# Row convolutions four rows at a time, six tiles of exponentials added in DRAM, one bank drained by VectorE

## The chip, the cores and the metric

One core of one Trainium2 chip runs the whole kernel. The metric is the device time of one execution in microseconds (us); three runs of the kernel before gave a median of 1929.07 us (1928.27 to 1931.76).

## The reference

Eight images of 64 channels and 64 x 64 pixels pass two layers.

```python
# layer 0: attention over the 4096 pixels of each image, plus a unary term
q, k, v = wq @ x + bq, wk @ x + bk, wv @ x + bv
q, k = q - mean(q), k - mean(k)
out = softmax(q.T @ k / 8) applied to v
out = out + sum over pixels of softmax(mean(q) . k) * v
x = x + out
# layer 1: three binary convolutions of the same x, summed, gated
s = sum over k in (1, 3, 5) of batchnorm(conv(sign(x + move_k), mean|w_k| * sign(w_k - mean w_k)) + cb_k)
gate = sigmoid(grouped product of mean(s) over pixels with gw, + gb), channels shuffled
return s * gate + x
```

Signs are +1 and -1, so each convolution is a sum of small integers, times one factor per output channel.

## The kernel before, in words

Images are worked in four pairs: 128 partitions are 64 channels of one image and 64 of the other. A pair has eight blocks of 512 pixels (8 rows of the image), so the kernel has 32 blocks, numbered g. A block has 32 steps, numbered j; each takes 128 pixels as keys.

**A step** (`scores`, `weighted`, `summed`; loop in `attend`). TensorE (PE) makes the scores of both images, four fp32 products of 64 x 64 weights and 512 columns, one in each quarter of its array. ScalarE (ACT) takes their exponential out of PSUM into a tile e (`L485`), 128 x 1024 fp32; e comes from a pool `ep` of five buffers, which it shares with the gather's tile `parts`. One step later PE multiplies e by the values (`L493`) into the two banks `acc`, and VectorE (DVE) adds e to `es` (`L506`, `L508`). Every fp32 product is two instructions on PE. Scores use a ring of two double banks of PSUM (`ps_s`), `acc` has one pair (`ps_a`), and everything else shares two banks (`ps_m`, `m_tile`).

**What hangs on the steps.** `plan(g)` gives each step of block g a list of further work; every engine takes its instructions in the order in which the program emits them, and DMAs issued on SP or POOL are taken in order too. At step 0 of a block:
- `weighted_out` (`L516`): ACT copies both banks of the block before to SBUF;
- `send` (`L523`) and `gather` (`L531`): es goes to DRAM and comes back in another arrangement, in four transfers on SP; `fold_first`, `fold`, `fold_last` and `spread` (steps 3 to 6) add the rest, take reciprocals and send them to all partitions; `added`, `finish` (12, 13) make the layer's output; `signs_wide`, `signs` (15, 17, 19) its signs;
- `mix_rows`: on PE, the queries of the next block (`L460`) and the convolutions of the block three before.

**The convolutions, two rows at a time.** `row_sums` and `row_sums3` (steps 17 and 19) make sums and differences of rows of signs on VectorE; SP copies what the other half of the partitions needs. Products (`row_product`, `L704`) then work on half as many rows: A, B, S and D, four for 3x3 of 3 taps each; for 5x5 A, B and S with 10 taps and D with 5. One product has 64 x 64 bf16 weights and 256 columns (four rows of 64). The order on PE is made in `mix_rows`: one sequence for each half of the partitions (row group), the two images side by side; the 3x3 follows eight of the products of S and the 1x1 (`L787`). `begin_rows` (`L730`) and `hold_rows` (`L737`) on ACT take the 1x1 and the 3x3 out of PSUM at the end of `mix_rows`; `add_rows` (`L746`, `L752`) on DVE adds the 5x5, `add_halves` (`L759`) and `end_rows` (`L765`) follow at steps 7 to 10.

The weights of S and D are made once, in block 2 (`weight_combinations`). The last block and what comes after it use another path (`mix`), one product for each tap. The values of the next pair (`values`, `L313`) are made in the second half of a pair's blocks.

Of the kernel before, what the change touches and what calls it, by code (L numbers as in the profile page):

```python
# [26 lines left out]
P = 128  # L27
# [12 lines left out]
FIRST = [0, 1, 10, 35]  # L40
LOW, HIGH = 1e-20, 1e20
# [3 lines left out]
def conv_seq_kernel(ctx, tc, x, wq, wk, wv, vecs, w1, w3, w5, wtap, gw, out):  # L45
# [44 lines left out]
    def load_weights():  # L90
# [7 lines left out]
        for h in range(2):  # L98
# [22 lines left out]

    wc = {
        k: cp.tile([P, k // 2 + 1, k * C], BF16, tag=f"wc{k}", name=f"wc{k}") for k in KS[1:]
    }


# [5 lines left out]
            cp.tile([P if o == 0 else C, HH + k - 1, HH + k - 1], BF16, tag=f"s{k}{o}", name=f"s{k}{o}")  # L132
            for o in range(2 if k == 3 else 1)
# [62 lines left out]
    frac = {k: cp.tile([P, 3], F32, tag=f"frac{k}", name=f"frac{k}") for k in KS[1:]}  # L196
# [3 lines left out]
    def norms():  # L200
        nc.vector.reciprocal(inv, inv)
        nc.vector.tensor_tensor(inv, inv, gamma, ALU.mult)
        nc.vector.tensor_tensor(scale, inv, sf, ALU.mult)
        for n in (1, 2):
            for i, f in enumerate((0.5, -0.5, -1.0)):
                nc.vector.tensor_scalar(
                    frac[KS[n]][:, i : i + 1], scale[:, n : n + 1], f, None, ALU.mult
                )
        nc.vector.tensor_tensor(sh3, cb, rm, ALU.subtract)
        nc.vector.tensor_tensor(sh3, sh3, inv, ALU.mult)  # L210
        nc.vector.tensor_tensor(sh3, sh3, beta, ALU.add)
        nc.vector.tensor_reduce(shift, sh3, AX.X, ALU.add)
# [32 lines left out]
    def n_products(k, name):  # L245
        return k if k == 3 or name == "D" else 2 * k

    def weight_combinations(k):
        tt, w, g = nc.vector.tensor_tensor, wc[k], [tap_row(k, r) for r in range(k)]
        tt(w[:, 1, :], g[0], g[2], ALU.add)  # L250
        tt(w[:, 0, :], w[:, 1, :], g[1], ALU.add)
        tt(w[:, 1, :], g[1], w[:, 1, :], ALU.subtract)
        if k == 5:
            tt(w[:, 2, :], g[3], g[4], ALU.add)
            nc.vector.tensor_scalar(w[:, 2, :], w[:, 2, :], 2.0, None, ALU.mult)

    class Pair:
# [3 lines left out]
        def __init__(self, name, xt):  # L261
            self.name, self.x = name, xt
            self.xs = sm.tile([P, 8], F32, tag="xs", name=f"xs_{name}")
            self.q, self.x2, self.s, self.y1, self.acc = {}, {}, {}, {}, {}
            self.es, self.r, self.joint, self.sc, self.gap = {}, {}, None, None, None
# [235 lines left out]
        def summed(self, qb, j, e):  # L501
            if j == 0:
# [7 lines left out]
        def weighted_out(self, qb, parts=(slice(0, QB),)):  # L510

            acc = self.acc[qb]
            self.acc[qb] = self.tile(fp, "o", qb, (P, 2, QB))
            for c in parts:
                for h in range(2):
                    nc.scalar.copy(self.acc[qb][:, h, c], acc[h][:, c])  # L516
# [3 lines left out]

        def send(self, qb):
            self.sent = self.tile(dp, "es", qb, (4, 32, 4, QB // 2))
            nc.sync.dma_start(  # L523
                out=self.sent.rearrange("g i q c -> (g i) (q c)"),
                in_=self.es.pop(qb).rearrange("p b c -> p (b c)"),
            )
# [52 lines left out]
        def added(self, qb, cols=slice(0, QB)):  # L579
# [3 lines left out]
            nc.vector.tensor_tensor(self.x2[qb][:, cols], acc[:, 0, cols], acc[:, 1, cols], ALU.add)  # L583
# [12 lines left out]
        def join(self):  # L596
# [32 lines left out]
        def copy_tile(self):  # L629
# [3 lines left out]
            for r in (0, W5 - 2):  # L633
                nc.vector.memset(self.sc[:, r : r + 2, :], 0.0)

        def copy_signs(self, qb, n, r0, r1, copies):
            rows = slice(qb * ROWS + r0 + pads[n], qb * ROWS + r1 + pads[n])
            for b in range(2):
                if self.sc is not None and n == 2:
                    copies[b](out=self.sc[img[1 - b], rows, :], in_=sy[n][0][img[b], rows, :])  # L640
                elif self.sc is not None and b == 1:
                    copies[b](out=sy[n][1][:, rows, :], in_=sy[n][0][img[b], rows, :])
# [7 lines left out]
        def row_sums(self, qb):  # L650


            r0 = qb * ROWS
            tt, y5 = nc.vector.tensor_tensor, sy[2][0]
            e5 = self.tile(fp, "e5", qb, (P, 22, W5), BF16)
            e3 = self.tile(fp, "e3", qb, (P, 16, W3), BF16)


            ec = self.tile(fp, "ec", qb, (P, 8 * W5 + 16 * W3), BF16)
            c0 = ec[img[0], 0 : 8 * W5].rearrange("p (r w) -> p r w", w=W5)  # L660
            c1 = ec[img[1], 0 : 18 * W5].rearrange("p (r w) -> p r w", w=W5)
            c3 = ec[img[0], 8 * W5 :].rearrange("p (r w) -> p r w", w=W3)
            self.rows_of_sums = e5, e3, c0, c1, c3
            tt(e5[:, 0:8, :], y5[:, r0 : r0 + 8, :], y5[:, r0 + 2 : r0 + 10, :], ALU.subtract)
            tt(e5[:, 8:18, :], y5[:, r0 + 1 : r0 + 11, :], y5[:, r0 + 2 : r0 + 12, :], ALU.subtract)
            tt(e5[:, 18:22, :], y5[:, r0 + 1 : r0 + 8 : 2, :], y5[:, r0 + 2 : r0 + 9 : 2, :], ALU.add)
            nc.sync.dma_start(out=c1, in_=e5[img[0], 0:18, :])
            nc.sync.dma_start(out=c0[:, 0:4, :], in_=e5[img[1], 18:22, :])
            nc.sync.dma_start(out=c0[:, 4:8, :], in_=y5[img[1], r0 + 4 : r0 + 11 : 2, :])

        def row_sums3(self, qb):
            r0 = qb * ROWS
            tt, y3 = nc.vector.tensor_tensor, sy[1][0]
            _, e3, _, _, c3 = self.rows_of_sums
            tt(e3[:, 0:8, :], y3[:, r0 : r0 + 8, :], y3[:, r0 + 2 : r0 + 10, :], ALU.subtract)
            odd, even = y3[:, r0 + 1 : r0 + 8 : 2, :], y3[:, r0 + 2 : r0 + 9 : 2, :]
            tt(e3[:, 8:12, :], odd, even, ALU.subtract)
            tt(e3[:, 12:16, :], odd, even, ALU.add)
            nc.sync.dma_start(out=c3, in_=e3[img[1]])

        def row_product(self, z, b, k, name, i, r0):

            e5, e3, c0, c1, c3 = self.rows_of_sums
            half, c = divmod(i, k)
            h = 1 if k == 5 and name != "S" else 0
            taps = {
                "A": (tap_row(k, 0), tap_row(k, min(3, k - 1))),
                "B": (tap_row(k, 2), tap_row(k, k - 1)),
                "D": (wc[k][:, 1, :],),
                "S": (wc[k][:, 0, :], wc[k][:, k // 2, :]),  # L690
            }[name][half]
            if k == 3:
                first, step = {"A": (0, 2), "B": (1, 2), "D": (8, 1), "S": (12, 1)}[name]
                src = e3[img[0]] if b == 0 else c3
            elif h == 1:
                first, step = {"A": (0, 10), "B": (1, 11), "D": (8,)}[name][half], 2
                src = e5[img[1]] if b == 1 else c1
            elif b == 1:
                first, step, src = 4 * half, 1, c0
            elif half == 0:  # L700
                first, step, src = 18, 1, e5[img[0]]
            else:
                first, step, src = r0 + 4, 2, sy[2][0][img[0]]
            nc.tensor.matmul(  # L704
                z[img[b], :].rearrange("p (h w) -> p h w", w=HH),
                taps[img[h], c * C : c * C + C],
                src[:, first : first + 3 * step + 1 : step, c : c + HH],
                start=(i == 0),
                stop=(i == n_products(k, name) - 1),
# [12 lines left out]
        def row_sets(self, qb):  # L722

            sv = self.s[qb].rearrange("p (j t w) -> p j t w", t=2, w=HH)
            return sv[:, :, 0, :], sv[:, :, 1, :]

        def begin_rows(self, qb, z):

            self.s[qb] = self.sum_tile(qb)
            nc.scalar.activation(self.s[qb], z, AF.Identity, bias=shift, scale=scale[:, 0:1])  # L730

        def hold_rows(self, qb, two, i):

            if i == 0:
                self.zh, self.z3 = self.tile(sm, "es", f"z3_{qb}", (P, 2, QB)), []
            z = self.zh[:, i, :]
            nc.scalar.activation(z, two, AF.Identity, scale=frac[3][:, 0:1])  # L737
            self.z3 += [
                z[:, bass.ts(t, QB // 2)].rearrange("p (j w) -> p j w", w=HH) for t in range(2)
            ]  # L740

        def add_rows(self, qb, a, b, s):

            for out, z, by in zip(self.row_sets(qb), (a, b), (scale[:, 2:3], frac[5][:, 2:3])):
                z = z.rearrange("p (j w) -> p j w", w=HH)
                nc.vector.scalar_tensor_tensor(out, z, by, out, ALU.mult, ALU.add)  # L746
            self.join_halves(2, s)

        def join_halves(self, i, z):
            t = self.z3[i]  # L750
            z = z.rearrange("p (j w) -> p j w", w=HH)
            nc.vector.scalar_tensor_tensor(t, z, frac[5][:, 0:1], t, ALU.mult, ALU.add)  # L752

        def add_halves(self, qb, i):

            if i == 3:
                self.join_halves(3, self.z5d)
            for t, out in enumerate(self.row_sets(qb)):
# [536 lines left out]
```

## Time and profile before

| what | value |
|---|---|
| median of three runs | 1929.07 us |
| the profiled execution | 1928.49 us, of which the span 1926.3 |
| granted TensorE clock | 0.997 |
| exponentials on ACT, `L485` | 1024 of 1024 ns |
| additions to es on DVE, `L508` | 960 of 1220 ns |
| row products on PE, `L704` | 2726 of 270 ns, overlapping |
| scores and weighted products on PE | 8192 and 8192 instructions of 590 ns, overlapping |
| DMA | 80.58 MB, one queue busy 13.1% of 16 engines' span |

The span goes from the first to the last instruction; the profiled execution's time has 2.2 us around it. Matmuls are pipelined, so the duration of one on PE is not what it costs: four of them run at once in quarters of the array, and the next starts before one ends. How often they start is read from the timeline. A row of the timeline is start, duration, engine, line, operation, output and input, count.

### The profile page before, as it was taken

The numbers are of one execution on the slowest core, as the hardware profiler recorded it, in microseconds if no ns is written. First come the engines' busy times: TensorE is split into PE (matmuls) and PEld (weight loads), VectorE is DVE, ScalarE is ACT, GpSimd is POOL, SyncE is SP. The second block draws the span as 40 slices with busy tenths as digits, with TensorE's granted clock in tenths as the row PEclk, the third lists the DMA queues.
The fourth block names the chain that finished last, engine by engine and source line by source line (L and its number), as shares of the span: only waits on it lengthen the run. The fifth ranks groups of instructions, "written<-read, shape, count | busy, mean of one in ns | idle before, by whom it ended". The sixth has DMA issues, their size and how long they took to land.

```text
span 1926.3 us, 48418 instructions
## 1 busy us (share of the span) xinstructions
PE 1908.6 (99%) x20848; PEld 954.7 (50%) x20848; DVE 1592.5 (83%) x2066; ACT 1277.6 (66%) x1585; POOL 5.9 (0%) x26
## 2 busy tenths in 40 slices
PE   9999999999999999999999999999999999999997
PEld 4333544444356453454435545444544555666664
DVE  6878888889887888888888888898887888877876
ACT  5667766666666766666666676666666666666663
POOL 0000000000000000000000000000000000000000
PEclk9999999999999999999999999999999999999998
DMA  3021110110102111111101211011111011111011
GB/s 101 32 65 33 30 40 32 40 35 16 41 32 84 57 49 29 41 32 40 35 15 41 81 56 57 27 30 41 32 40 35 16 57 48 52 39 39 23 35 46
DMA packets 58998, 80.58 MB, mean 42 GB/s; under 512 B 15628, under 2 KB 40600, under 8 KB 58648
## 3 DMA queue, kind: packets, MB, share of 16 engines
q1 hardware_dynamic: 58024, 76.22, 13.1%
q8 instruction: 165, 2.70, 0.6%
q10 hardware_dynamic: 720, 1.18, 0.2%
q14 instruction: 57, 0.47, 0.1%
q0 software_dynamic: 32, 0.01, 0.0%
HBM read 39.27 MB, written 24.77 MB: 33 GB/s over the span
## 4 chain that ended last, share of the span: by engine, by line
PE 97%; DVE 1%; ACT 1%; DMA 0%; issue 0%; SPq 0%; DVEq 0%
PE ps L474 46%; PE acc L493 45%; PE z L704 4%; PE pv L313 1%; PE pq L460 1%; PE z L787 1%; DMA x<-in_x 0%; ACT e L485 0%; DVE es L508 0%; PE z_5d L704 0%; PE warm L155 0%; DVE r L577 0%; DVE sb L829 0%; ACT rc_ck L418 0%; DVE es_j L829 0%
## 5 line engine op out<-in xcount | busy, mean ns | idle before, releaser
L485 ACT ACTIVATE e<-ps 128x1024 f32<-128x1024 f32 x1024 | 1048.5, 1024 | 605.4 <-PE ps L474 588.8
L508 DVE TENSOR_TENSOR es<-es,e 128x1024 f32<-128x1024 f32 x960 | 1171.5, 1220 | 182.3 <-ACT e L485 152.9
L474 PE MATMUL ps<-q,x 64*64 64x512 f32 x8192 | 1136.7, 590 | 0.9 <-DVE kb L165 0.9
L493 PE MATMUL acc<-e,v 64*64 64x512 f32 x8192 | 1133.8, 589 | 0.6 <-ACT e L485 0.3
L474 PEld LDWEIGHTS ps<-q,x 64*64 64x64 f32 x8192 | 434.7, 133 | 407.4 <-issue 190.8
L493 PEld LDWEIGHTS acc<-e,v 64*64 64x64 f32 x8192 | 379.1, 131 | 501.3 <-ACT e L485 301.6
L704 PE MATMUL z<-ec,wt 64*64 64x256 bf16 x754 | 69.1, 270 | 0.0
L704 PE MATMUL z<-e,wt 64*64 64x256 bf16 x754 | 69.1, 270 | 0.0
L746 DVE SCALAR_TENSOR_TENSOR sb<-z,scale,sb 128x256 f32<-128x256 f32 x29 | 14.0, 484 | 65.7 <-PE z L704 65.7
L704 PEld LDWEIGHTS <-wt 64*64 64x64 bf16 x1508 | 65.0, 105 | 0.1
L506 DVE TENSOR_TENSOR es<-e,e 128x1024 f32<-128x1024 f32 x32 | 39.2, 1226 | 26.8 <-ACT e L485 26.8
L704 PE MATMUL z<-ec,wc 64*64 64x256 bf16 x464 | 60.5, 270 | 0.0
L704 PEld LDWEIGHTS <-wc 64*64 64x64 bf16 x1218 | 57.5, 106 | 3.1
L620 ACT ACTIVATE s<-x,vec 128x512 bf16<-128x512 f32 (+2 forms) x66 | 46.2, 702 | 5.1 <-DVE x L588 5.1
L759 DVE TENSOR_TENSOR sb<-sb,es_z 128x256 f32<-128x256 f32 x116 | 43.9, 420 | 1.0
L704 PE MATMUL z<-e,wc 64*64 64x256 bf16 x319 | 44.4, 270 | 0.0
L737 ACT ACTIVATE es_z<-z,frac 128x512 f32<-128x512 f32 x58 | 39.1, 687 | 0.0
L516 ACT COPY o<-acc 128x512 f32<-128x512 f32 (+2 forms) x66 | 34.4, 580 | 1.2 <-PE acc L493 1.2
L313 PEld LDWEIGHTS pv<-wx,x 64*64 64x64 f32 x1024 | 23.6, 134 | 15.8 <-issue 8.2
L467 DVE TENSOR_SCALAR q<-pq,mx 128x256 f32<-128x256 f32 x30 | 14.5, 484 | 19.7 <-PE pq L460 19.7
L704 PE MATMUL z<-s,wc 64*64 64x256 bf16 x145 | 25.4, 270 | 0.0
L588 DVE SCALAR_TENSOR_TENSOR x<-x,ou,x 128x512 f32<-128x512 f32 (+2 forms) x33 | 24.3, 736 | 1.2
(156 smaller groups left out, 752.6 us busy)
## 6 DMA issues: line engine op xcount, KB each, us to landing
es<-es SPq DMA_DIRECT2D x31, 512.0 KB
e_parts<-es SPq DMA_DIRECT2D x124, 128.0 KB
r<-rc SPq DMA_DIRECT2D x62, 128.0 KB
x<-in_x SPq DMA_DIRECT2D x15, 512.0 KB
out<-sb SPq DMA_DIRECT2D x28, 256.0 KB
ec<-e SPq DMA_DIRECT2D x29, 153.0 KB
xc<-in_x SPq DMA_DIRECT2D x60, 64.0 KB
ec<-e SPq DMA_DIRECT2D x29, 132.0 KB
```

What stands on the lines that cost most here:

```text
L313: nc.tensor.matmul(pv[img[h], b, i * w : (i + 1) * w], self.x[img[b], bass.ds((4 * g + i) * P + h * H, H)], self.wx[img[b], :], start=True ...
L474: nc.tensor.matmul(ps[img[h], b, :], self.x[img[b], bass.ds(j * P + h * H, H)], self.q[qb][img[b], :], start=True, stop=neg is None,)
L485: nc.scalar.activation(e, ps, AF.Exp, scale=1.0 / 8.0)
L493: nc.tensor.matmul(self.acc[qb][h][img[b], :], self.v[img[h], j, img[b]], e[img[h], b, :], start=(j == 0), stop=(j == NK - 1),)
L506: nc.vector.tensor_tensor(self.es[qb], self.first, e, ALU.add)
L508: nc.vector.tensor_tensor(self.es[qb], self.es[qb], e, ALU.add)
L516: nc.scalar.copy(self.acc[qb][:, h, c], acc[h][:, c])
L588: nc.vector.scalar_tensor_tensor(x2, x2, self.ou, self.x[:, bass.ts(qb, QB)][:, cols], ALU.add, ALU.add)
L620: nc.scalar.activation(sy[n][0][:, rows, pad : pad + HH], self.x2[qb][:, r0 * HH : r1 * HH].rearrange("p (h w) -> p h w", w=HH), AF.Sign, ...
L704: nc.tensor.matmul(z[img[b], :].rearrange("p (h w) -> p h w", w=HH), taps[img[h], c * C : c * C + C], src[:, first : first + 3 * step + 1 ...
L737: nc.scalar.activation(z, two, AF.Identity, scale=frac[3][:, 0:1])
L759: nc.vector.tensor_tensor(out, out, self.z3[i], ALU.subtract if (i, t) == (3, 1) else ALU.add)
```

## The change

**Four rows at a time.** Four output rows come from combinations of six (3x3) or eight (5x5) rows of signs, and as many products of 3 or 5 taps, each with combined weights. A product now has 128 columns: 64 pixels of the first and the second four rows of the block. The factors are small whole numbers, exact in bf16; the fractions (1/24, 1/360, 1/45) lie in the scale on the way out. `row_sums` becomes `row_step` in seven parts on VectorE (steps 17 to 24), with copies at 21 and 24. Out of PSUM: `hold` on ACT (3x3, and products 4 and 5 of the 5x5), `join` on DVE, then `sums_of_pairs`, `odd_powers` (ACT), `end_products`, `add_pair` at steps 2 to 9. `begin_rows` moves to step 1, the folds and `spread` two steps later, the unary products and the means' scores from step 0 to step 1.

**Sums in DRAM.** In blocks 0 to 30, tiles 4, 9, 14, 19, 24 and 28 of e aren't added by VectorE. The first is written to DRAM by SP; the others, and then es, are added to it there by transfers that POOL issues.

**One bank by VectorE.** `weighted_out` copies the second bank on DVE.

```diff
+DRAM_TILES = (4, 9, 14, 19, 24, 28)
...
-        def summed(self, qb, j, e):
-            if j == 0:
+        def summed(self, qb, j, e, dram=False):
+            if dram and j in DRAM_TILES:
+                self.add_in_dram(qb, e, j == DRAM_TILES[0])
+            elif j == 0:
...
-                for h in range(2):
-                    nc.scalar.copy(self.acc[qb][:, h, c], acc[h][:, c])
+                nc.scalar.copy(self.acc[qb][0][:, c], acc[0][:, c])
+                nc.vector.tensor_copy(self.acc[qb][1][:, c], acc[1][:, c])
...
+        def add_in_dram(self, qb, e, first=False):
+            if first:
+                self.sent = self.tile(dp, "es", qb, (4, 32, 4, QB // 2))
+            out = self.sent.rearrange("g i q c -> (g i) (q c)")
+            e = e.rearrange("p b c -> p (b c)")
+            if first:
+                nc.sync.dma_start(out=out, in_=e)
+            else:
+                nc.gpsimd.dma_start(out=out, in_=e, accum_op=ALU.add)
...
         def send(self, qb):
+            self.add_in_dram(qb, self.es.pop(qb))
...
+        def combine(self, k, y, d, f, t):
+            def pairs(rows, r):
+                at = min(r, 2)
+                fours = rows[:, r - at : r - at + 8, :].rearrange("p (q f) w -> p q (f w)", f=4)
+                return fours[:, :, at * w : (at + 2) * w]
+            def plus_minus(i, a, by, b):
+                for r in range(2):
+                    out, op = t[:, i + 2 * r : i + 2 * r + 2, :], (ALU.add, ALU.subtract)[r]
+                    if by is None:
+                        tt(out, a, b, op)
+                    else:
+                        stt(out, a, by, b, ALU.mult, op)
+            if k == 5:
+                def differences():
+                    tt(d, y[:, 0:10, :], y[:, 2:12, :], ALU.subtract)
+                    nc.vector.tensor_scalar(d4, d, 4.0, None, ALU.mult)
+                def first():
+                    tt(f[:, 0], pairs(d, 1), pairs(d4, 3), ALU.subtract)
+                    tt(f[:, 1], pairs(d4, 1), pairs(d, 3), ALU.subtract)
+                    tt(f[:, 2], pairs(d4, 1), pairs(d4, 3), ALU.subtract)
+                def second():
+                    stt(f[:, 2], pairs(y, 3), -9.0, f[:, 2], ALU.mult, ALU.add)
+                    tt(f[:, 3], pairs(d4, 0), pairs(d4, 4), ALU.add)
+                def third():
+                    stt(ends(f), pairs(d, 2), -17.0, f[:, 3], ALU.mult, ALU.add)
+                    plus_minus(0, one(2, 1), None, one(2, 0))
+                def fourth():
+                    for r in range(2):
+                        stt(t[:, 4 + 2 * r : 6 + 2 * r, :], one(0, 0), 2.0 - 4.0 * r, one(0, 1), ALU.mult, ALU.add)
+                    plus_minus(8, one(1, 1), 2.0, one(1, 0))
...
             nc.tensor.matmul(
-                z[img[b], :].rearrange("p (h w) -> p h w", w=HH),
-                taps[img[h], c * C : c * C + C],
-                src[:, first : first + 3 * step + 1 : step, c : c + HH],
+                z[img[b], :].rearrange("p (q w) -> p q w", w=HH),
+                wc[k][img[h], n, c * C : c * C + C],
+                src[:, first : first + step + 1 : step, c : c + HH],
...
-            S = products(5, "S")
-            three = [t for name in "ABSD" for t in products(3, name)]
-            seqs[0] += S[:8] + [((1,), 0, 1.0)] + three + S[8:]
-            seqs[1] += products(5, "A") + products(5, "B") + products(5, "D")
+            seqs[0] += products(5, 4) + products(3, 4, 5, 0, 1, 2, 3) + [((1,), 0, 1.0)] + products(5, 5)
+            seqs[1] += products(5, 0, 1, 2, 3, 6, 7)
...
+            elif n == (3, 5):
+                p.hold(acc[1][:, 0 : 4 * HH], 6, 2, 0)
+            elif n == (3, 3):
+                p.hold(acc[0], 0, 4, 0)
         if c is not None:
+            p.hold(banks5[0][:, 0 : 4 * HH], 4, 2, 2)
+            p.join(ends[:, 0 : 4 * HH], 6, 2)
+            p.join(banks5[1], 0, 4)
...
+                put(1, p3.begin_rows, b3)
+                put(2, p3.sums_of_pairs)
+                put(3, p3.odd_powers)
+                put(3, p3.end_products, b3)
+                put(4, p3.add_pair, b3, 0)
+                put(8, p3.add_pair, b3, 1)
+                put(9, p3.add_pair, b3, 2)
...
+                for i in range(5):
+                    put(17 + i, p2.row_step, b2, 5, i)
+                put(21, p2.row_copies, 5)
+                for i in range(2):
+                    put(22 + 2 * i, p2.row_step, b2, 3, i)
+                put(24, p2.row_copies, 3)
```

Of the functions not shown, `sums_of_pairs` is two fp32 tensor_tensor of 384 elements a partition, `odd_powers` two ACT instructions of 128, `end_products` two scalar_tensor_tensor of 128, each `add_pair` two of 256; a 3x3's `row_step` is a subtraction of 528 elements and six instructions of 132 or 264.

## The prediction

> **What bounds the kernel now.** I read the engines' busy times first, then the chain of work that ended last, then the waits, then the timeline of one block boundary.
>
> ```profile
> PE 1908.6 (99%) x20848; PEld 954.7 (50%) x20848; DVE 1592.5 (83%) x2066; ACT 1277.6 (66%) x1585; POOL 5.9 (0%) x26
> ...
> PE 97%; DVE 1%; ACT 1%; DMA 0%; issue 0%; SPq 0%; DVEq 0%
> ```
>
> The chain runs 97% through PE: only PE's time, or a new wait put in front of PE, moves the end. The waits agree: ACT stands idle 589 us for PE's scores, and DVE 153 us for ACT's exponentials.
>
> ```profile
> ACT e L485 <- PE ps L474: 588.8, 891, 3.1
> DVE es L508 <- ACT e L485: 152.9, 329, 1.0
> SPq L531 <- DMA es<-es: 73.0, 30, 3.0
> ```
>
> The boundary, from PE's timeline around 1014 us. Queries start at 1014.42, row products at 1014.85, the next scores at 1017.51; from there half a step costs 0.86 us (a step of 1.72 us: four scores and four weighted products, each written as two instructions).
>
> ```profile
> 1014.42 0.38 PE L460 MATMUL pq<-x,mm 64*64 64x256 f32 x1
> ...
> 1014.85 0.27 PE L704 MATMUL z<-e,wc 64*64 64x256 bf16 x1
> ...
> 1014.96 0.27 PE L704 MATMUL z<-e,wc 64*64 64x256 bf16 x1
> ...
> 1017.51 0.60 PE L474 MATMUL ps<-q,x 64*64 64x512 f32 x2
> ...
> 1018.37 1.16 PE L493 MATMUL acc<-e,v 64*64 64x512 f32 x8
> ```
>
> So the row products hold PE for 2.66 us in each of 29 blocks, 77 us of the span. That is what the change can win from.
>
> **Row products.** Before: 94 products of 256 columns and two 1x1 products of 512 (50 products on row group 1, 44 plus the 1x1 on group 0, two images side by side). A group of four, one per quarter of the array, starts every 0.11 us (1014.85, 1014.96), so 25 groups x 0.11 = 2.7 us, as seen. After: 8x5 + 6x3 = 58 products per image, 116 of 128 columns. Group 0 carries 5+18+5 = 28 of them per image and the 1x1, group 1 carries 30. The page has no 128-column bf16 product. By columns it costs 0.055 us (half of 0.11); if weight loads set the pace (they take 105 ns each) it stays at 0.11. The nearest row is the value product, 65 fp32 columns with one weight load each:
>
> ```profile
> 937.89 0.29 PE L313 MATMUL pv<-wx,x 64*64 64x65 f32 x8
> 937.89 0.59 PE L313 MATMUL pv<-wx,x 64*64 64x65 f32 x28
> ```
>
> Those are the same stretch, read up to two moments: 20 more products in 0.30 us, 0.06 per group of four, with as many loads and nearly the length in time of 128 bf16 columns (512 fp32 columns take 0.43 us a group, so 65 take 0.055). I take 0.058. Group 0 then needs 28 x 0.058 + 0.22 (1x1) = 1.84 us against 2.66, a gain of 0.8.
>
> The Trainium skill, "TensorE: Matmul & The Clock Gate", section "Back-to-back issue gap", speaks against this: it gives about 81 ns per product at 128 columns in a stream with weight loads. At 81 ns the gain after the wait below would be an estimated 0.03 us a block and the forecast 1928; no row here shows quarter-array products so slow.
>
> **VectorE drains one bank.** The 3x3 now comes after only five 5x5 groups (1014.85 + 5 x 0.058 = 1015.14) and writes first the bank that VectorE drains; before, eight 5x5 products and the 1x1 lay ahead of it. The last weighted products end at 1014.60. A VectorE copy of 512 fp32 columns from PSUM isn't shown; copies of 192 (358 ns) and 128 (292 ns) give 0.69. It ends near 1015.36, so PE, whose queue is in order, stands until about 1015.40: 0.25 us. The other bank, ACT's (1014.73 + 0.59), is free by then. Remaining on group 0: 23 x 0.058 + 0.22 = 1.55, and scores start at 1016.95 instead of 1017.51. **Gain 0.56 us a block, 29 blocks: 16 us.** Without the wait it is 0.81 and 23.5 us.
>
> What is late next? ACT does copy, query (0.50), a hold of 256 columns, one of 512 (0.69, from about 1016.65 to 1017.35), one of 256: all done by 1017.8, and weighted products need the banks at 1017.81. On VectorE the joins (0.48 + 0.75) run from 1017.0 to 1018.2; the scores that need their bank again come at 1018.67. No new wait, by 0.4 us. begin_rows (0.78) moves to step 1 into ACT's idle 0.69 there; PE waits for an exponential only 0.45 after its end (1013.11 against 1013.56), so it stays hidden. odd_powers (two of some 0.3) fits in step 3.
>
> **VectorE's sum.** Per block: six es additions go, 6 x 1.22 = -7.3. Row combinations: additions at the rows of their sizes (680: 0.505; 528: 0.43; 272: 0.29; 136 by slope 0.22), scalar_tensor_tensor on bf16 is not shown, between that 0.29 and the fp32 0.42, I take the latter: 6.8 against 2.2, +4.6. Joins and adding out: 5.6 against 4.6, +1.0. Copy +0.7. Sum -1.1: VectorE stays near 49 us of a block of 58. In the first ten steps it has about 18.3 us of work in 17.2, a lag of 1 us, and a buffer of exponentials is written again only four or five steps (6.9 or 8.6 us) later. At steps 17 to 25 of blocks with values it lags 2 us at most. Hidden. ACT +0.3 a block, hidden by its idle 0.69 per step.
>
> **Sums in DRAM.** Six tiles a block leave by DMA: tile 4 as a plain transfer on SP, tiles 9 to 28 and es itself as accumulating ones on POOL, which has nothing else queued. Each waits for the one before. Tile j's buffer is written again by exponential j+5 (the gather's tile takes one buffer until step 7, so tile 4's by j+4). From the end of e_9 to the start of e_14 there are 5 x 1.72 - 1.02 = 7.57 us, and PE has 0.45 to spare: a transfer may take **8.0 us**. Beyond that each of tiles 9, 14, 19, 24 stalls ACT, then PE, in 31 blocks: 124 us per us. No accumulating transfer is in the trace. From below, the plain es (same bytes, SP) took 3.45 us from issue to the gather that waits for it:
>
> ```profile
> 1014.40 0.34 SPq L523 DMA_DIRECT2D es<-es  x1
> 1017.85 1.73 SPq L531 DMA_DIRECT2D e_parts<-es  x4
> ```
>
> From above, by the list of DMA issues (size, us to landing), the one transfer that POOL issued took 5.9 us for 10 KB, at the start of the program: 5.9 + 3.45 = 9.35.
>
> ```profile
> vec<-in_vecs POOLq DMA_DIRECT2D x1, 10.5 KB, 5.9
> ```
>
> The nearest row is the plain send; for the read beside the write I double it, **6.9**, and the cost is nothing. "DMA: Bandwidth & Descriptors" of the Trainium skill, section "Specifications", gives a first byte of about 1 us for GpSimd's transfers against 0.6 for SP's, which would make the doubled transfer an estimated 7.3 us, under 8.0 too; the row of 5.9 us stands against it.
>
> The gather waits for the accumulated es: 1014.4 + 0.6 (tile 28's landing) + 6.9, four issues of 1.73 in all, some 2 us to land: 1025.6, where fold_first, moved from step 3 to 5, comes at about 1025.1. Half a us of VectorE's slack. Behind the gather on SP are the query copies and tile 4, due at 1024.2, issued 1025, landed by 1028.7 where e_8 writes at 1030. Where the next image loads (three blocks, 4 x 512 KB ahead of tile 4) I charge 2 us in all. The unary products moved to step 1 give back about 1 us, the parallel drain in the tail 0.3.
>
> **Sum.** The profiled execution took 1928.49 us (span 1926.3). 1928.5 - 16.2 + 2 - 1.3 = 1913.0; the median of the runs shown is 0.6 above it: **1913.5**.
>
> **Rivals.**
> 1. The accumulating transfer takes longer than 8.0 us. For: POOL's 5.9 us for 10 KB, and a read and a write for every byte. Against: that one ran while the inputs loaded; twice the plain send is 6.9. It decides from 8.0 + 16/124 = 8.13 us on. At 8.5 us: 1913 + 62 = 1975; at 9.35: 2080. Slower. The part of the interval 3.45 to 9.35 above 8.13 is 21%; with what POOL's own work may add, 23%.
> 2. Weight loads or instructions set the pace of short products. At 0.11 the end moves to 1018.15, +0.64 a block: 1947, slower (5%); near 0.08 nothing is left: 1927, no change. Against: 0.06 in the value products.
> 3. VectorE is behind at a block's end, so its drain is late and PE stands at the 3x3; each 0.1 us takes 2.9 us of the gain, and 0.5 us late gives 1928. Against: VectorE waited 0.7 us for the query products in each of 29 blocks. Together with 2 in the middle: 10%, no change.
>
> ```profile
> DVE q L467 <- PE pq L460: 19.7, 29, 0.7
> ```
>
> **Numbers.** A measurement of this kernel tells about 0.2% (4 us) from no change. Forecast 62%, its own range 1903 (no wait at the 3x3) to 1923; no change 10%; slower 28% (23 + 5). The range reaches to 1975, the transfer of 8.5 us, and takes in 1947: about 3% lie below it and 13% above.
>
> **What would show it.** Right: the time from the first row product to the next scores is 2.1 us, with a hole of some 0.25 before the 3x3; rounds of four 0.058 apart; the step stays 1.72 at e_14, e_19, e_24, e_29; VectorE still near 83%. Wrong: ACT's exponentials waiting for a DMA; a step longer than 1.72 every fifth; row products 0.08 or more apart; VectorE's idle before its additions gone.

## The result and the profile after

The changed kernel takes 1929.45 us (median of 12 runs, 1927.09 to 1935.89), the kernel before 1929.32 in the same series: ratio 1.0003, 95% interval [0.9994, 1.0012]. No difference, where 1913.5 was forecast; that gain and loss cancel so exactly is chance. The profiled execution took 1928.91 us, of which the span is 1927.1.

First the engines' busy times and the chain of work that ended last, on the page of the changed kernel.

```profile
PE 1891.6 (98%) x21486; PEld 798.8 (41%) x21486; DVE 1517.0 (79%) x2423; ACT 1279.8 (66%) x1639; POOL 165.7 (9%) x208
...
PE 49%; DMA 1%; DVE 1%; ACT 0%; issue 0%; SPq 0%; ACTq 0%
```

PE has 17 us less work and VectorE 75 us less, and still the span is as long. The chain's shares add up to 51%: followed back from the end it stops at 920.92 us, at an accumulating transfer of tile 9, and on its way it passes others. These are pieces of it (start, length, what).

```profile
920.92 8.13 DMA es<-e
...
1089.48 6.97 DMA es<-e
...
1273.89 8.09 DMA es<-e
```

Before, the chain had no DMA worth a percent. The list of waits (total, times, longest) says the same:

```profile
ACT e L502 <- PE ps L491: 549.6, 851, 3.1
ACT e L502 <- DMA es<-e: 22.9, 8, 7.6
```

ACT waited 22.9 us for transfers of es, in eight places; before, in none. It wants to write an exponential into a buffer that a DMA still reads.

**The part that went as forecast.** PE's timeline at the boundary of block 17: queries, row products, the next scores.

```profile
1019.91 0.38 PE L477 MATMUL pq<-x,mm 64*64 64x256 f32 x1
...
1020.35 0.22 PE L798 MATMUL z<-ec,wc 64*64 64x128 bf16 x2
...
1020.41 0.22 PE L798 MATMUL z<-ec,wc 64*64 64x128 bf16 x2
...
1020.47 0.22 PE L798 MATMUL z<-ec,wc 64*64 64x128 bf16 x2
...
1020.59 0.55 PE L798 MATMUL z<-t,wc 64*64 64x128 bf16 x2
1020.94 0.24 PE L798 MATMUL z<-ec,wc 64*64 64x128 bf16 x1
...
1022.38 0.64 PE L491 MATMUL ps<-q,x 64*64 64x512 f32 x2
```

Rounds of four start 0.06 us apart. Between 1020.59 and 1020.94 no product starts: PE stands some 0.3 us for the 3x3's bank. From the first row product to the next scores 2.03 us pass; before, 2.66.

**Where it was given back.** I took the time from the first exponential of a block to that of the next, from the starts of `L485` and `L502` in the two traces (us):

| block | before | after | difference |
|---|---|---|---|
| 9, 17, 25 (nothing special) | 58.13 | 57.47 | -0.66 |
| 5, 6, 22 (values of the next pair) | 59.17 | 58.55 | -0.61 |
| 2 (image load) | 57.03 | 62.21 | +5.18 |
| 10 (image load) | 58.63 | 66.29 | +7.66 |
| 18 (image load) | 58.63 | 61.11 | +2.48 |
| 7, 13, 15, 21 (exponential 14 late) | 59.17 | 59.01 to 59.53 | -0.15 to +0.36 |

The three blocks that load the next pair's images cost 15.3 us more than before; the other blocks from 0 to 30 together cost 14.1 less. That is nearly the whole result: some 0.6 us won in each ordinary block, lost again in three.

Block 10, first SP's queue before (the block's first exponential at 601.04), then SP's queue and ACT in the changed kernel (first exponential at 600.80):

```profile
604.55 1.74 SPq L531 DMA_DIRECT2D e_parts<-es  x4
606.34 1.85 SPq L70 DMA_DIRECT2D x<-in_x  x4
```

```profile
609.34 1.74 SPq L557 DMA_DIRECT2D e_parts<-es  x4
611.12 1.85 SPq L71 DMA_DIRECT2D x<-in_x  x4
613.07 2.25 SPq L468 DMA_DIRECT2D xc<-in_x  x2
615.41 0.58 SPq L547 DMA_DIRECT2D es<-e  x1
```

```profile
615.36 1.02 ACT L502 ACTIVATE e<-ps 128x1024 f32<-128x1024 f32 x1 [0.69 <-PE ps L491]
624.00 1.94 ACT L502 ACTIVATE e<-ps 128x1024 f32<-128x1024 f32 x2 [7.61 <-DMA es<-e]
```

Now the gather waits until the accumulated sum has landed, so it and the image come 5.0 us later in the block. Tile 4 is issued behind both, at 615.41, and lands near 624, 8.6 us later. Exponential 8 writes into tile 4's buffer, and ACT stands 7.61 us for it. The next view counts engines in stretches of this time (start:end, length, busy time and instructions of PE, PEld, DVE, ACT, POOL, then the granted TensorE clock, the share of the DMA engines, GB/s).

```profile
617.00:618.00 1.00, 1.00 (x13) 0.40 (x8) 0.96 (x3) 0.00 (x0) 0.00 (x0) 1.00 0.97 291
618.00:620.00 2.00, 0.74 (x8) 0.00 (x0) 1.97 (x5) 0.00 (x0) 0.00 (x0) 1.00 1.02 351
...
622.00:624.00 2.00, 0.00 (x0) 0.00 (x0) 0.00 (x0) 0.00 (x1) 0.00 (x0) 0.50 0.19 73
...
626.00:627.00 1.00, 1.00 (x12) 0.39 (x8) 0.97 (x5) 0.21 (x2) 0.77 (x1) 0.50 0.00 0
```

The DMA engines are full until 620. And while PE stands, its granted clock falls to 0.50 and stays there until about 628.7, so the first products after the stand are slow too: the step to exponential 10 is 2.2 us too long, after 6.9 at exponential 8.

### The profile page after: what moved, and what is told of

The parts are those of the page before. It is cut to its first block, busy times and chain, and to the rows that moved or that the text cites. A ratio compares the mean times of both kernels' runs of the same rounds, so it can differ in the third digit from the quotient of the medians.

```text
span 1927.1 us, 50314 instructions
## 1 busy us (share of the span) xinstructions
PE 1891.6 (98%) x21486; PEld 798.8 (41%) x21486; DVE 1517.0 (79%) x2423; ACT 1279.8 (66%) x1639; POOL 165.7 (9%) x208
## 4 chain that ended last, share of the span: by engine, by line
PE 49%; DMA 1%; DVE 1%; ACT 0%; issue 0%; SPq 0%; ACTq 0%
PE ps L491 23%; PE acc L510 23%; DMA es<-e 1%; PE z L798 1%; DVE o L536 1%; PE z L885 0%; PE z_5e L798 0%; ACT e L502 0%; PE pv L330 0%; PE pre L1243 0%; DVE r L603 0%; ACT rc_ck L435 0%; DVE es L528 0%; SPq L468 0%; PE su L596 0%
## 5 line engine op out<-in xcount | busy, mean ns | idle before, releaser
L502 ACT ACTIVATE e<-ps 128x1024 f32<-128x1024 f32 x1024 | 1049.1, 1025 | 590.9 <-PE ps L491 549.6
L528 DVE TENSOR_TENSOR es<-es,e 128x1024 f32<-128x1024 f32 x774 | 943.8, 1219 | 265.5 <-ACT e L502 260.3
L510 PE MATMUL acc<-e,v 64*64 64x512 f32 x8192 | 1089.8, 590 | 13.1 <-ACT e L502 12.9
L491 PE MATMUL ps<-q,x 64*64 64x512 f32 x8192 | 1093.1, 591 | 3.5 <-ACT e L502 2.6
L510 PEld LDWEIGHTS acc<-e,v 64*64 64x64 f32 x8192 | 333.7, 131 | 561.3 <-ACT e L502 321.5
L491 PEld LDWEIGHTS ps<-q,x 64*64 64x64 f32 x8192 | 350.1, 133 | 489.5 <-issue 346.3
L549 POOL DMA_DIRECT2D es<-e x155 | 133.7, 863 | 1499.5 <-ACT e L502 954.9
L865 DVE SCALAR_TENSOR_TENSOR sb<-pt,sb 128x256 f32<-128x256 f32 x174 | 65.9, 420 | 0.0
L798 PE MATMUL z<-t,wc 64*64 64x128 bf16 x1392 | 60.6, 217 | 3.9 <-DVE o L536 0.5
L798 PE MATMUL z<-ec,wc 64*64 64x128 bf16 x1392 | 61.6, 217 | 0.0
L828 ACT ACTIVATE pt<-z,frac 128x256 f32<-128x256 f32 (+1 forms) x87 | 44.3, 543 | 15.6 <-PE z L798 15.6
```

Source lines behind the costliest of these rows:

```text
L491: nc.tensor.matmul(ps[img[h], b, :], self.x[img[b], bass.ds(j * P + h * H, H)], self.q[qb][img[b], :], start=True, stop=neg is None,)
L502: nc.scalar.activation(e, ps, AF.Exp, scale=1.0 / 8.0)
L510: nc.tensor.matmul(self.acc[qb][h][img[b], :], self.v[img[h], j, img[b]], e[img[h], b, :], start=(j == 0), stop=(j == NK - 1),)
L528: nc.vector.tensor_tensor(self.es[qb], self.es[qb], e, ALU.add)
L549: nc.gpsimd.dma_start(out=out, in_=e, accum_op=ALU.add)
L798: nc.tensor.matmul(z[img[b], :].rearrange("p (q w) -> p q w", w=HH), wc[k][img[h], n, c * C : c * C + C], src[:, first : first + step + 1 ...
```

## The experiments

My theory: each part of the change does what it should, and what it wins is lost where tile 4's transfer meets the image load. Rivals were that VectorE's relief or the accumulating transfers cost something everywhere. All ratios below are against the kernel before, which took 1928.5 to 1929.1 us in these series.

**e1_spread.** The image's four transfers are written into the program one by one, every fourth step from step 6, instead of all at step 1.

```diff
-                    put(1, begin)
+                    put(6, begin)
+                    for c in range(4):
+                        put(6 + 4 * c, part, c)
```

> The four transfers of the next image leave at steps 6, 10, 14 and 18 of their block instead of all at step 1; nothing else differs from the changed kernel. Theory A: the row products' gain of some 0.66 us a block arrived, and three blocks (2, 10, 18) gave 17 us back, because tile 4, a plain transfer on SP, is queued behind the gather and 2 MB of image, and e_8 waits for its buffer. Then these three blocks fall to about 57.5 us and the time to 1912 us. Rival B: the accumulating transfers cost something everywhere, so where the image is loaded matters little: 1926 to 1930 us.

Measured: 1914.79 us, ratio 0.9919 [0.9903, 0.9936]. Most of the loss is gone: the three blocks cost 2.5 us more than before, not 15.3. What is left sits elsewhere. SP's queue held the pieces up behind `spread`: in blocks 10 and 18 they left as one, two together and one (608.65, 617.02, 627.10 in block 10), in block 2 as one and three. The two together ran beside tile 9's accumulating transfer (issued at 617.06), which took 9.5 us in block 10 and 8.7 in block 18, the next one beside tile 14's (7.9 in both). Against e2_keep4, exponential 14 is 1.8 and 1.0 us late there and exponential 19 another 1.0 and 1.1; blocks 10 and 18 are 2.2 and 1.5 us longer.

**e2_keep4.** In the three blocks with an image load VectorE adds tile 4, and the sum in DRAM begins with tile 9.

```diff
+                    tiles = DRAM_TILES[1:] if qb == 2 and pr + 1 < n_pairs else DRAM_TILES
```

> In the three blocks that load an image, tile 4 is added by VectorE and tile 9 is the first to go to DRAM; the image is still loaded at step 1. Theory A (tile 4's place in SP's queue): as without the crowding, 1912 to 1915 us. Rival C: it is the image's traffic itself that slows the transfers of these blocks, whichever tile: less than 5 us gained, 1925 us or more.

Measured: 1911.83 us, ratio 0.9907 [0.9890, 0.9923]. Three tiles of 186 decide over the change; whether the order on SP or the image's traffic holds tile 4 back, this run doesn't tell (e10_poolq does). The three blocks take 57.20, 57.96 and 57.95 us, 1.2 less than before together. Exponential 14 is still late in blocks 13 and 15, by 1.2 and 0.4 us.

**e6_dramonly.** The kernel before with the sums in DRAM alone; rows, and the drain of both banks by ACT, as before.

```diff
+                self.add_in_dram(qb, e, j == DRAM_TILES[0])
```

> The kernel before with the sums in DRAM alone (the folds, the spread and the checks one or two steps later, as in the changed kernel); rows by twos, both banks drained by ACT. Theory A: only the three image blocks lose, 17 us together: 1946 us, and all other blocks as before. Rival B: a loss in every block as well, 1950 us or more.

Measured: 1944.98 us, ratio 1.0080 [1.0059, 1.0102]. Blocks 2, 10 and 18 cost 5.9, 3.7 and 6.7 us more than before, 16.3 together; the other 28 together 0.8. VectorE's share falls from 83% to 71%, and no ordinary block is shorter for it: off the path that sets the end, the relief is worth nothing there. By itself this part of the change is slower.

**e3_nodram.** The changed kernel without sums in DRAM.

```diff
-                    pending[0].summed(*pending[1:], g < n_blocks - 1)
+                    pending[0].summed(*pending[1:])
```

> All tiles of exponentials are added by VectorE, es is sent by a plain transfer on SP; the rows by fours and VectorE's drain stay. If VectorE has room, the loss in the three image blocks goes and nothing comes instead: 1911 us. Rival D: with 7.3 us more VectorE has 56 us of work in a block of 57.5, and 59 in one of 58.5 where values are made; it falls behind, exponentials wait for buffers and the 3x3 for VectorE's drain: 1925 us or more, with waits of ACT for VectorE in the blocks with values.

Measured: 1919.96 us, ratio 0.9951 [0.9935, 0.9968], between the two forecasts. VectorE is 90% busy. Ordinary blocks and those with values keep their whole gain (57.47, 58.50). The loss is in a few: block 3 takes 63.79 us, 6.3 more than in the changed kernel, at its first step; against e2_keep4 block 2 loses 1.2 and blocks 8, 16 and 24 lose 0.8 each. In block 3 the third rival of the prediction is seen: VectorE, behind with the weight combinations of block 2, drains its bank late, and the 3x3 waits 3.8 us; the granted clock is then 0.50 from 193.4 to 200.2, which makes the loss larger than the stand. In blocks 8, 16 and 24 the same wait is 0.9 us.

```profile
PE z L798 <- DVE o L536: 7.9, 8, 3.8
```

So the sums in DRAM save 9.8 us in five blocks against e2_keep4, and 8 in all, since without them exponential 14 is on time in blocks 13 and 15.

**e10_poolq.** The changed kernel, but tile 4's plain transfer is issued by GpSimd, so that it isn't behind the gather and the image in SP's order.

```diff
-                nc.sync.dma_start(out=out, in_=e)
+                nc.gpsimd.dma_start(out=out, in_=e)
```

> The changed kernel with one line different: the plain transfer that begins the sum in DRAM (tile 4) is issued by GpSimd, not by SP, in all blocks. It is no longer behind the late gather and the image's four 512 KB loads in SP's order; the image still loads at the same step. Theory 1 (the order on SP's queue holds tile 4 back): blocks 2, 10 and 18 lose less than 1.5 us each against their neighbours, 1912 to 1915. Theory 2 (2 MB of image fill the DMA engines, whoever issues tile 4): e_8 still stands 4 us and more in those blocks, 1922 to 1929. Between the two: the issue was late by the 4.8 us of the gather, the rest is traffic.

Measured: 1926.29 us, ratio 0.9985 [0.9976, 0.9995]. In block 10 tile 4 is issued at 610.25, 10.8 us after the block's first exponential and not 14.6. Exponential 8 is 3.8 to 3.9 us late all the same in each of the three blocks, which cost 12.8 us more than before. The second theory holds: the traffic is the cause. The order on SP made it worse in block 10 alone, where exponential 8 was 6.9 us late in the changed kernel; in blocks 2 and 18 it was 3.8 and 3.5. An image issued ahead of the gather was not tried. The summary of this line's transfers shows the same transfer alone and in traffic:

```profile
L547 POOL DMA_DIRECT2D es<-e x31: 560/560/580, 24.8 to 1783.3; - x31
...
DMA to landing us min/median/max: 2.9/3.0/9.7
```

3.0 us in ordinary blocks, up to 9.7 beside 2 MB of image.

**e8_keep4_act.** e2_keep4, and ACT drains both banks as before.

```diff
-                nc.vector.tensor_copy(self.acc[qb][1][:, c], acc[1][:, c])
+                nc.scalar.copy(self.acc[qb][1][:, c], acc[1][:, c])
```

> e2_keep4 with the third part of the change undone: ScalarE drains both banks of weighted products, as before the change. Theory (the 3x3 waits for the drain of the second bank, and two copies of about 0.59 us one after the other on ScalarE end 0.4 to 0.5 us later than VectorE's one of 0.68 beside ScalarE's): the hole grows from 0.3 to about 0.75 us in 29 blocks, 12 to 13 us more: 1924. Rival (VectorE's drain costs as much as it saves, since VectorE also has joins and sums to make): within 3 us of 1911.8.

Measured: 1921.62 us, ratio 0.9961 [0.9947, 0.9975], 9.8 more than e2_keep4. The stand ahead of the 3x3 grows from 0.3 to 0.7 us, and each block's first step by 0.41 us, 11.9 in 29 blocks; 1.6 come back, since exponential 14 is on time in blocks 13 and 15. With the new order of the products VectorE's drain is needed.

**e7_keep4_hole.** e2_keep4 with the 5x5's kinds 4 and 5 ahead of the 3x3, to fill the stand, and their hold right behind them.

```diff
-            seqs[0] += products(5, 4) + products(3, 4, 5, 0, 1, 2, 3) + [((1,), 0, 1.0)] + products(5, 5)
+            seqs[0] += products(5, 4, 5) + products(3, 4, 5, 0, 1, 2, 3) + [((1,), 0, 1.0)]
...
+            elif n == (5, 5):
+                p.hold(banks5[0][:, 0 : 4 * HH], 4, 2, 2)
```

> e2_keep4 with the order of the row products changed: both 5x5 rounds that read sums (fourth and fifth kinds) come ahead of the 3x3, and the hold of their bank follows the last 5x5 product. In the changed kernel TensorE stands some 0.29 to 0.35 us ahead of the 3x3, since only five groups of four lie between the last weighted products and VectorE's drain of its bank (675 ns). With ten groups of 0.058 us, 0.58 us, ahead of it the stand should be gone. Theory (the hole is the drain): 0.29 x 29 blocks = 8.4 us less than e2_keep4's 1911.8, so 1903.4. Rival (the hole covers something else, such as the second hold or the score banks, which is then late in its place): within 2 us of 1911.8.

Measured: 1922.82 us, ratio 0.9966 [0.9954, 0.9979]: 11 us worse, not 8 better. PE's timeline shows a new wait in place of the old one.

```profile
1011.64 0.22 PE L798 MATMUL z<-ec,wc 64*64 64x128 bf16 x1
1012.42 0.21 PE L798 MATMUL z<-t,wc 64*64 64x128 bf16 x1 [0.56 <-ACT pt L828]
```

PE waits for the hold that I had moved ahead, though the hold reads only sums that are finished.

**e11_order.** The same with the hold written after the 3x3's first kind.

```diff
-            elif n == (5, 5):
+            elif n == (3, 4):
```

> e7_keep4_hole with one line moved: the hold of the fourth and fifth 5x5 sums is written after the 3x3's first kind of products, not before it. In e7_keep4_hole the 3x3 waited 0.56 us for that hold (ScalarE, 1.82 to 2.29 us after the first exponential of the block, the 3x3 at 2.34), though it reads nothing of it; VectorE's drain had ended at 1.57. Theory (the wait came from the place of the hold in the order of the program; the hole of e2_keep4 is VectorE's drain): ten groups of 0.058 us end at 1.62 and the 3x3 follows at once; with five groups fewer behind it 0.29 us a block go, 8.4 us: 1903.4. Rival (the 3x3's banks are free only when ScalarE is through with more than its copy, wherever the hold is written): 0.5 us and more again, 1918 to 1923.

Measured: 1923.30 us, ratio 0.9974 [0.9964, 0.9984]; the theory's 1903.4 was not reached. The time is near the rival's, but not for the rival's reason, since the 3x3's bank was free: now 50 row products ran ahead of the stand, the 3x3's first kind among them, where e7_keep4_hole had 38. So PE waits at whatever comes next after the hold in the order of the program. Next on the other row group are products into the second bank of the same two-bank tile that the hold reads.

**e12_order_only.** Only the order of the products; all holds and joins where e2_keep4 has them.

```diff
-            seqs[0] += products(5, 4) + products(3, 4, 5, 0, 1, 2, 3) + [((1,), 0, 1.0)] + products(5, 5)
+            seqs[0] += products(5, 4, 5) + products(3, 4, 5, 0, 1, 2, 3) + [((1,), 0, 1.0)]
```

> e2_keep4 with the order of the products alone changed: the 5x5 kinds 4 and 5 ahead of the 3x3, every hold and join written where e2_keep4 has them. In e11_order 52 products ran, the first kind of the 3x3 among them, before TensorE stood for the hold; so it wasn't the 3x3's bank that was waited for. Row group 1 writes its kinds 0 to 3 into the other half of the two-bank tile whose first half the hold reads. Theory (a write into one half of a tile waits for a read of the other half that is written earlier in the program; with the hold behind the last product nothing waits, and VectorE's drain ends at 1.57, before ten groups are through at 1.62): no stand, 0.29 us a block less than e2_keep4, 1903.4. Rival (the 3x3 after ten groups waits for ScalarE in any order, or the last hold and the joins, now all behind the end of the products, hold up the scores): 1911 to 1923.

Measured: 1908.56 us, ratio 0.9897 [0.9881, 0.9914]: the lowest of all, but 3.3 us below e2_keep4 and not 8.4. The two intervals overlap, so the difference is read from the blocks. The stand is gone, and the first step is 0.29 us shorter in most blocks, as expected. In ordinary blocks the next step takes 0.24 of it back (57.42 against 57.47). VectorE's rows at that boundary, of e12_order_only, show why:

```profile
1005.50 0.48 DVE L833 SCALAR_TENSOR_TENSOR pt<-z_5e,frac,pt 128x256 f32<-128x256 f32 x1 [1.24 <-PE z_5e L798]
1006.25 0.75 DVE L833 SCALAR_TENSOR_TENSOR pt<-z,frac,pt 128x512 f32<-128x512 f32 x1 [0.27 <-ACT pt L828]
```

The second join waits for ACT's last hold and ends 4.7 us after the block's first exponential, as in e2_keep4; the scores that need its bank start at 4.77, there at 4.81. The holds and joins now set that place. Blocks 4, 8, 12, 16, 20 and 24, whose second step is long anyway, keep the 0.29. So the new order itself is worth some 2.6 us; another 1.6 of the 4.3 us between the two profiled executions is exponential 14 on time in blocks 13 and 15. That a write into one half of the tile waits for a read of the other half is what the three runs agree with; it was not tried with two separate tiles.

**e9_few.** e7_keep4_hole with sums in DRAM only in blocks 2, 3, 8, 16 and 24.

```diff
+                    pending[0].summed(*pending[1:], tiles if g in (2, 3, 8, 16, 24) else ())
```

> e7_keep4_hole with sums in DRAM only in blocks 2, 3, 8, 16 and 24, those in which the kernel without sums in DRAM lost time or came in late from the block ahead; everywhere else VectorE adds all tiles. Theory (the sums in DRAM pay only where VectorE is full, and the accumulating transfers, 7.7 to 8.1 us long now and then, cost the odd 0.5 to 1.2 us elsewhere): 1 to 2 us below e7_keep4_hole, 1902. Rival (without the relief VectorE drains late in other blocks too, now that TensorE comes to the 3x3 with no hole to spare): 4 to 10 us above e7_keep4_hole.

Measured: 1923.07 us, ratio 0.9969 [0.9958, 0.9979], the same as e7_keep4_hole (1922.82). Neither forecast held: with VectorE at 88% hardly anything is late (0.4 us in block 1), and nothing is won. Sums in DRAM pay in five blocks; elsewhere they are neutral, but for the image loads and an exponential 14 that is late now and then.

## Why the prediction was wrong, by its own steps

**Row products: right.** 0.058 us per round of four was forecast and 0.06 measured; 2.03 us from the first product to the scores against 2.1, a stand of 0.3 against 0.25, a gain of 0.66 us per ordinary block against 0.56. Rival 2 is out. The Trainium skill's figure of 81 ns per product at 128 columns ("TensorE: Matmul & The Clock Gate", "Back-to-back issue gap") doesn't hold for these products in quarters of the array, each with its weight load.

**VectorE drains one bank: right.** e8_keep4_act prices its absence at 0.41 us a block. Rival 3 appeared only with the sums in DRAM taken out, in blocks 3, 8, 16 and 24 of e3_nodram.

**No new wait from holds and joins, "by 0.4 us": right in sign, too large.** The joins end 0.1 us before the scores need their bank. e12_order_only used that up at once.

**VectorE's sum: right in sign.** The share went from 83% to 79%, some 2.4 us a block where 1.1 was forecast, and cost nothing in ordinary blocks (e6_dramonly: 71% and no gain).

**The accumulating transfer: estimated 6.9 us, limit 8.0.** From the list of DMA issues of the changed kernel:

```profile
es<-e POOLq DMA_DIRECT2D x155, 512.0 KB, 5.4
```

The median is 5.4, 1.8 times the 3.0 of the plain one of GpSimd (e10_poolq): doubling was about right, the base of 3.45 too high. Rival 1 as a general case is out. But the time is not one number: it reached 8.1 us, and in blocks 7, 13, 15 and 21 exponential 14 was 0.5 to 0.9 us late, 3.3 us together that I had at nothing. The limit was smaller than forecast, too: a transfer of 7.67 us (block 7) already made exponential 14 0.46 us late, so it was about 7.2 and not 8.0. In these four blocks tile 9's transfer meets `spread`, as in block 15:

```profile
920.45 1.11 SPq L586 DMA_DIRECT2D r<-rc  x2
920.92 0.86 POOL L549 DMA_DIRECT2D es<-e  x1 [17.58 <-ACT ck L435]
929.16 1.02 ACT L502 ACTIVATE e<-ps 128x1024 f32<-128x1024 f32 x1 [1.66 <-DMA es<-e]
```

In the changed kernel's trace tile 9 took 6.2 to 8.1 us in the eight blocks where the reads of `spread` (r<-rc) were issued within 0.5 us of it, and 5.2 to 5.6 where they were issued 1.1 us or more ahead; in block 19, where they came 0.7 us behind, it took 5.5. `spread` was late in the four blocks, where the transfer of es at step 0 had taken 6.2 to 7.0 us. What slowed that one is open, and no run moved `spread` to test this.

**"Where the next image loads (three blocks, 4 x 512 KB ahead of tile 4) I charge 2 us in all": this step failed.** Measured: 15.3 us more than before in the three blocks, and 1.3 of gain that blocks 10 and 18 would have had (block 2 has no row products yet): 16.6 instead of 2. Against e2_keep4 the same blocks lose 16.5. I had the place and the order, and put no time of the image's own transfers to it. I took tile 4's landing from an ordinary block (issued 1025, landed by 1028.7, due 1030) and left out that the image's 2 MB go through the same DMA engines. The trace of before could have priced it: those engines moved 188 and 274 GB/s in the two stretches of 6 us around the image load of block 10 (columns as above).

```profile
604.00:610.00 6.00, 6.00 (x86) 4.05 (x80) 3.75 (x6) 4.00 (x6) 0.00 (x0) 1.00 0.66 188
610.00:616.00 6.00, 6.00 (x62) 3.81 (x57) 5.79 (x10) 3.50 (x4) 0.00 (x0) 1.00 0.72 274
```

By these rates I estimate 8 to 11 us for 2 MB ahead of tile 4. Counted from its issue at 1025 tile 4 lands at 1033 to 1036, 3 to 6 us after 1030: 9 to 18 us in three blocks, where 16.6 were measured (some 3 of them by the clock) and 2 were written.

The sum then closes: with 16.6 in place of 2, and 3.3 for exponential 14, the forecast 1913.0 becomes 1930.9; the gain of 0.61 to 0.66 in place of 0.56, in 29 blocks, takes some 2.3 off again. That makes 1928.6, and the profiled execution took 1928.91.

**The clock** was not in the forecast at all. After two of the three stands it was 0.50, and the step to exponential 10 was 2.2 and 2.0 us too long, against 0.5 after the third, with the clock at 1.00: some 1.5 to 1.7 us each.

## What to carry to other kernels

A transfer on the critical path is priced in the blocks with the heaviest traffic, not in the ordinary ones: bytes ahead of it over the measured GB/s, from the moment when the first of them can start, against the step that needs its buffer back. When a large change moves the time by nothing, compare the period block by block: here most blocks won and three lost, and leaving three tiles of 186 to VectorE turned no change into 0.9% (e2_keep4). A gain on the engine that sets the end holds only up to the next thing that is nearly late, so write its slack down too.

## What the runs showed of the hardware

- The changed kernel's PE stood still for 6.34 us (block 10), 3.33 (block 2) and 2.93 (block 18). Its granted clock was 0.50 from 621.8 to 628.7 and from 150.8 to 154.2, and a group of eight score instructions spanned 1.93 us where 1.09 is usual; with the third it stayed at 1.00. Length alone doesn't decide: in e10_poolq stands of 3.30 and 3.21 us brought 0.50 and one of 3.37 didn't, in e6_dramonly one of 3.50 didn't. What decides can be read from the times. The changes of clock lie on a grid of 3.413 us (150.81 and 621.85 are 138 such stretches apart), and half clock lasted one or two stretches (3.41 or 6.83 us). In the changed kernel, e10_poolq, e6_dramonly and e3_nodram, each of the seven falls to 0.50 in blocks 1 to 30 came at the end of a stretch in which PE had been idle for 2.5 us or more by the profile. The three stands that left the clock alone (2.93, 3.37 and 3.50 us) lay across two stretches, with at most 2.0 us in either. The Trainium skill ("TensorE: Matmul & The Clock Gate", "What's actually happening") gives an idle window of about 3.4 us that runs freely; length and free run agree with these traces, where 2.5 us of idle time in a window were enough.
- A 512 KB accumulating transfer from SBUF to DRAM by GpSimd lands in 5.4 us (5.1 to 8.1; 9.5 beside two pieces of an image in e1_spread), a plain one in 3.0; each of the first holds GpSimd 0.86 us, of the second 0.56. VectorE's additions beside them kept their time (1219 ns against 1220).
